# Output projections of a two-layer graph transformer in seven half-size products, and the attention of two batches taken together

## The chip, the cores and the metric

The kernel runs on one core of a Trainium2 chip. The metric is device time in microseconds (us), and lower is better. The engines are named as the profile names them: PE (TensorE, matrix products), PEld (its weight loads), DVE (VectorE), ACT (ScalarE), POOL (GpSimd) and SP (SyncE, which here issues every DMA). Every engine takes its instructions in the order in which the program lists them, and waits at each for the semaphores that it needs.

## The reference, cut to what matters

There are 128 batches of 128 nodes with 512 features, all in float32. Layer 0 is multi-head attention with 4 heads of 64 under an adjacency mask; layer 1 is a layer norm followed by attention with 8 heads of 64 under the mask with its diagonal set. Each layer adds its input to its output and normalises the sum.

```python
q, k, v = split_heads(x @ Wq), split_heads(x @ Wk), split_heads(x @ Wv)   # 4 heads (layer 0), 8 (layer 1)
sim = where(mask, einsum('bhid,bhjd->bhij', q, k) * scale, very_negative)
out = einsum('bhij,bhjd->bhid', softmax(sim), v)        # attention output, 256 or 512 wide
x = layernorm(x + out.reshape(B, N, INNER) @ Wo + bo)   # output product: 256 or 512 -> 512
```

The output product is the part that the change computes in another way. Per batch it multiplies 128 rows of 256 (layer 0) or 512 (layer 1) by a matrix with 512 columns.

## The kernel before, in words

**Groups and steps.** Two batches form a group g, and there are 64 groups. `step(s)` (L531) is called 67 times. In the steady state one step carries five groups' work at once: layer 0's q, k and v of group s (`product_0`, L337), layer 0's attention of group s-1, layer 1's q and k of group s-2 (`product("qk")`, L275), and layer 1's v and attention of group s-3 (`product("v")`). Within a step the attention is done twice, once per batch: `scores(k)` is called with k = 2s and k = 2s+1, and these two calls divide the step into a first and a second half.

**Products of two batches.** The projections to q, k and v use a seven-product scheme: the two batches' rows and the two halves of the columns make 2x2 blocks, and seven half-size products with sums of inputs and of weights take the place of eight. `sums` (L257) makes four sums of the inputs on POOL. Weight sums are made once. The products are numbered: 1, 6, 7 and 4 pile up in one PSUM bank ("a"), 5 and 3 in another ("f"), 2 has its own ("c"). Since a bank is read in between, the next product into it waits until DVE or ACT has read the one before it.

**Attention.** `scores` (L386) multiplies q and k into four PSUM banks (two per layer), POOL fills a tile `sm` with a very negative number (L410), DVE copies the scores into it under the mask (L412, two per layer; for layer 1 after merging the diagonal into the mask, L407) and takes the negative maximum of each row (L415). ACT takes the exponentials (`exps`, L424). `normalised` (L427) takes reciprocals of the sums on DVE (L432) and multiplies on POOL (L433). `blocks` (L436) transposes 32x32 blocks on DVE (L448) and sends them to DRAM, from where `probs_arrive` fetches them with four DMAs into their transposed place `pT`. `attend` (L458) multiplies with v and ACT copies the result to `aT` (L474).

**Output and norm.** `addend` (L476) adds the bias to the residual on POOL (in layer 1 after a scaling on ACT). `residual` (L487) makes the output product of one batch, with 512 columns (two matmuls in layer 0, four in layer 1), and DVE adds the addend (L499) and takes mean and variance (L501, L503); small POOL instructions make the root, and `norms` (L522) scales on DVE. Layer 1's result goes out by DMA. `turn` and `arrive` transpose a group's features by way of DRAM in the same way as the probabilities; `finish` (L245) and `in_order` (L235) put them in place on ACT, followed by the sums on POOL.

**What sets the order.** The tile framework's scheduling is off (`manual_schedule`): the order on each engine is that in which `step` calls these functions, and a helper that issues to DVE stands in DVE's queue where it was called. `exponentials` and `flush` empty lists of work put off, in the same way. [...]five rotate under the name "mm" (L50), three are fixed: "a", "a0" and a shared "f".

Of the kernel before, what the change touches and what calls it, by code (L numbers as in the profile page):

```python
# [27 lines left out]
def kernel(ctx: ExitStack, tc: tile.TileContext, x, adj, wq, wk, wv, wo, bo,  # L28
# [13 lines left out]
    four = ctx.enter_context(tc.tile_pool(name="four", bufs=4))  # L42
    dram = ctx.enter_context(tc.tile_pool(name="dram", bufs=2, space=bass.MemoryType.DRAM))
    ps_mm = ctx.enter_context(tc.tile_pool(name="ps_mm", bufs=5, space=PSUM))
# [20 lines left out]
    X, M = {}, {}  # L65

    def load(g):
        if g >= NG:
            return
        X[g] = four.tile([P, G, E], F32, tag="x", name=f"x_{g}")  # L70
        M[g] = four.tile([P, G, N], U8, tag="m", bufs=6, name=f"m_{g}")
        nc.sync.dma_start(X[g], x[g * G:(g + 1) * G].rearrange("b n e -> n b e"))
        nc.sync.dma_start(M[g], adj[g * G:(g + 1) * G].rearrange("b i j -> i b j"))
# [8 lines left out]
    mhalf = const.tile([P, 2], F32, name="mhalf")  # L82
# [25 lines left out]

    spare = []
    for tag, n in (("qk1", 4), ("v1", 2), ("xT1", 2), ("xs1", 2)):  # L110
        rows_n = one.tile([P, n, E], F32, tag=tag, name=f"raw_{tag}")
        spare.extend(rows_n[:, i] for i in range(n))

    def load_transposed(dst, src, name, scaled=0):
        rows, cols = src.shape
        raws = []
        for r in range(rows // P):
            if not spare:
                raw = three.tile([P, cols], F32, tag="h", bufs=7, name=f"{name}_{r}")
            else:  # L120
                raw = spare.pop(0)
            nc.sync.dma_start(raw, src[r * P:(r + 1) * P, :])
            raws.append(raw)
# [36 lines left out]
    def weight_sums():  # L160
        for w, ws in ((w1qk, wsqk), (w1v, wsv)):
            for c in range(KH):
                if w is w1qk:
                    b11, b12 = w[:, c, :, 0], w[:, c, :, 1]
                    b21, b22 = w[:, KH + c, :, 0], w[:, KH + c, :, 1]
                else:
                    b11, b12 = w[:, c, 0], w[:, c, 1]
                    b21, b22 = w[:, KH + c, 0], w[:, KH + c, 1]
                t2, t3, t4 = ws[:, 0, c], ws[:, 1, c], ws[:, 2, c]
                nc.vector.tensor_sub(t3, b22, b12)  # L170
                nc.vector.tensor_sub(b12, b12, b11)
                nc.vector.tensor_sub(t2, b22, b12)
                nc.vector.tensor_sub(t4, b21, t2)

    def weight_sums_0():
        b11, b12, b21, b22 = (w0[:, c:c + KH, h].rearrange("p c t f -> p c (t f)")
                              for c in (0, KH) for h in range(2))
        t2, t3, t4 = (ws0[:, i].rearrange("p c t f -> p c (t f)") for i in range(3))
# [4 lines left out]

    weight_sums_0()
    load_transposed(w1, w_qkv, "w_qkv", scaled=INNER[1])
    setup.append(turn_gamma_beta)
    load_transposed(wo1, w_out, "w_out")
    setup.append(weight_sums)

    WO = (wo0, wo1)  # L190
    RATIO, H, XT, QK, V, QKV = {}, {}, {}, {}, {}, {}
# [14 lines left out]
    TURNED, SCR, RAW = {}, {}, {}  # L206

    def turn(l, g, b):
        if not 0 <= g < NG:
            return  # L210
        if b == 0:
            TURNED[l] = one.tile([P, 4, G * KC * 32], F32, tag=f"turned{l}", name=f"turned{l}_{g}")
        src = X[g][:, b] if l == 0 else H[g, b]
        nc.vector.transpose(TURNED[l].rearrange("p a (b c i) -> p a b c i", b=G, c=KC)[:, :, b],
                            src.rearrange("p (c a i) -> p a c i", a=4, i=32))
        if b == G - 1:
            SCR[l] = put(TURNED[l], f"scr{l}_{g}")

    def arrive(l, g):
        if not 0 <= g < NG:  # L220
            return
        RAW[l] = one.tile([P, 4, G, KC, 32], F32, tag=f"raw{l}", name=f"raw{l}_{g}")
        fetch(RAW[l].rearrange("p a b c i -> p a (b c i)"), SCR[l])

    def first_transposed():
        xT = XT[0, 0] = one.tile([P, KC, T], F32, tag="xT0", name="xT0_0")
        for b in range(G):
            pt = mm_tile(f"xt_{b}")
            for c in range(KC):
                nc.tensor.transpose(pt[:, c * N:(c + 1) * N], X[0][:, b, c * P:(c + 1) * P], ident)  # L230
# [26 lines left out]
    def sums(l, g):  # L257
        xT = XT[l, g]
        xs = one.tile([P, 4, KH, N], F32, tag=f"xs{l}", name=f"xs{l}_{g}")
        a = xT.rearrange("p (h c) (b n) -> p b h c n", h=2, b=2)  # L260
# [6 lines left out]
        XS[l, g] = xs  # L267
# [69 lines left out]
    def product_0(g, *which):  # L337
# [5 lines left out]
        for i in which:  # L343
# [10 lines left out]
            elif first:  # L354
                tag = {"a": "a0", "f": "f"}[bank]
                ACC[0, bank] = ps_st.tile([P, 512], F32, tag=tag, name=f"{bank}0_{g}")
# [11 lines left out]
            if i in (1, 5, 6):  # L368
                e = one.tile([P, 512], F32, tag=("e5_0" if i == 5 else f"e{i}"), name=f"e0_{i}_{g}")
                EV[0, i] = e[:, :3 * P]  # L370
# [8 lines left out]
    SM, SUM, PT, AT, XB = {}, {}, {}, {}, {}  # L379
# [6 lines left out]
    def scores(k):  # L386
# [32 lines left out]
        exponentials(1)  # L419
# [16 lines left out]
    def blocks(k):  # L436
# [7 lines left out]
        pT = one.tile([P, 4, sum(HEADS), 32], F32, tag="pT", name=f"pT_{k}")  # L444
# [13 lines left out]
    def attend(k):  # L458
        both = members(k)
        if not both:  # L460
            return
        for l, g, b in both:
            K = HEADS[l] // 2
            pT = PT.pop((l, g, b))
            pm = mm_tile(f"av{l}_{g}_{b}")

            for h in range(HEADS[l]):
                s, kk = h % 2, h // 2
                o = pm[s * D:(s + 1) * D, kk * N:(kk + 1) * N]
                v = QKV[g][:, b, kk, 2, s * D:(s + 1) * D] if l == 0 else V[1, g][:, b, h * D:(h + 1) * D]  # L470
                nc.tensor.matmul(o.rearrange("p (a r) -> p a r", r=32), v, pT[:, :, s * K + kk, :],  # L471
                                 start=True, stop=True)
            AT[l, g, b] = two.tile([P, INNER[l]], F32, tag=f"aT{l}", name=f"aT{l}_{g}_{b}")
            nc.scalar.copy(AT[l, g, b], pm[:, :INNER[l]])  # L474

    def addend(l, k):  # L476

        for _, g, b in [m for m in members(k) if m[0] == l]:
            if l == 0:
                xin = X[g][:, b, :]  # L480
            else:
                xin = H.pop((g, b))
                nc.scalar.activation(xin, xin, AF.Copy, scale=RATIO.pop((g, b)))  # L483
            nc.gpsimd.tensor_tensor(xin, xin, (bias0, bias1)[l], op=ALU.add)  # L484
            XB[l, g, b] = xin

    def residual(l, k):  # L487
        for _, g, b in [m for m in members(k) if m[0] == l]:
            aT = AT.pop((l, g, b))
            nk = INNER[l] // P  # L490
            pm = mm_tile(f"o{l}_{g}_{b}")
            for c in range(nk):
                nc.tensor.matmul(pm, aT[:, c * P:(c + 1) * P], WO[l][:, c, :],  # L493
                                 start=(c == 0), stop=(c == nk - 1))
            if l == 0:
                y = three.tile([P, E], F32, tag="h", bufs=7, name=f"h_{g}_{b}")
            else:
                y = two.tile([P, E], F32, tag="y", name=f"y_{g}_{b}")
            nc.vector.tensor_add(y, pm, XB.pop((l, g, b)))  # L499
            st = three.tile([P, nc.vector.BN_STATS_DIM], F32, tag="st", name="st")  # L500
            nc.vector.bn_stats(st, y)  # L501
            mv = three.tile([P, nc.vector.BN_AGGR_DIM], F32, tag="mv", name=f"mv{l}_{g}_{b}")
            nc.vector.bn_aggr(mv, st)  # L503
            n = 2 - l
            ve = three.tile([P, 2], F32, tag="ve", name="ve")
            nc.gpsimd.tensor_scalar_add(ve[:, 0:1], mv[:, 1:2], EPS)  # L506
            if l == 0:


                nc.gpsimd.tensor_scalar(ve[:, 1:2], mv[:, 1:2], 1.0 + EPS, EPS * EPS,  # L510
                                        op0=ALU.mult, op1=ALU.add)
            r = three.tile([P, 2], F32, tag="rstd", name="rstd")
            nc.gpsimd.tensor_tensor(r[:, :n], ve[:, :n], mhalf[:, :n], op=ALU.pow)  # L513
            if l == 0:

                ratio = three.tile([P, 1], F32, tag="ratio", bufs=10, name=f"ratio_{g}_{b}")
                nc.gpsimd.tensor_scalar(ratio, ve[:, 1:2], r[:, 0:1], r[:, 1:2], op0=ALU.mult,
                                        op1=ALU.mult)
                RATIO[g, b] = ratio
            later.append(lambda: norms(l, g, b, y, mv, r))  # L520

    def norms(l, g, b, y, mv, r):  # L522
        n = 1 - l
        nc.vector.tensor_scalar(y, y, mv[:, 0:1], r[:, n:n + 1], op0=ALU.subtract, op1=ALU.mult)  # L524
        if l == 0:
            H[g, b] = y
        else:
            nc.sync.dma_start(out[g * G + b], y)


    def step(s):  # L531
# [6 lines left out]
        k = 2 * s  # L538
        scores(k)
        addend(0, k - 1)  # L540
        residual(1, k - 2)
        p("qk", 4, g=s - 3)
        exponentials()
        attend(k - 1)
        normalised(k)
        addend(1, k - 1)
        flush()
        turn(0, s + 1, 0)
        turn(0, s + 1, 1)
        product_0(s, 1, 5)  # L550
        p("", g=-1)
        blocks(k)
        arrive(0, s + 1)
        product_0(s, 2, 6)
        p("", g=-1)
        product_0(s, 3)
# [73 lines left out]
```

## Time and profile before

| | us |
|---|---|
| median of 3 runs (lowest, highest) | 2987.09 (2982.59, 2987.37) |
| the profiled execution, its own time | 2984.46 |
| its span, first to last instruction | 2982.70 |
| PE busy | 2920.0 (98%) |
| DVE busy | 1854.0 (62%) |
| POOL busy | 1567.4 (53%) |
| ACT busy | 1334.2 (45%) |
| TensorE clock granted (mean) | 0.994 |

The profile lists, for each group of instructions of one line and shape, how many there were, their busy time, the mean duration, and the idle time ahead of them with the engine that ended it. One float32 matmul shows as two records. Matmul records overlap in time, so the cost of one is read from start to start of neighbouring ones in the timeline, and not from its duration. In the steady state the two calls of `scores` start 45.14 us apart from step to step: from 145.58 us of the span (step 4) to 2854.3 us there are 60 such steps, the stretch ahead of them fills the pipeline, and the 128.4 us behind them drain it.

### The profile page before, as it was taken

The numbers are of one execution on the slowest core, as the hardware profiler recorded it, in microseconds if no ns is written. First come the engines' busy times: TensorE is split into PE (matmuls) and PEld (weight loads), VectorE is DVE, ScalarE is ACT, GpSimd is POOL, SyncE is SP. The second block draws the span as 40 slices with busy tenths as digits, with TensorE's granted clock in tenths as the row PEclk, the third lists the DMA queues.
The fourth block names the chain that finished last, engine by engine and source line by source line (L and its number), as shares of the span: only waits on it lengthen the run. The fifth ranks groups of instructions, "written<-read, shape, count | busy, mean of one in ns | idle before, by whom it ended". The sixth has DMA issues, their size and how long they took to land.

```text
span 2982.7 us, 59421 instructions
## 1 busy us (share of the span) xinstructions
PE 2920.0 (98%) x22089; PEld 2402.9 (81%) x22089; DVE 1854.0 (62%) x3291; ACT 1334.2 (45%) x4619; POOL 1567.4 (53%) x2055
## 2 busy tenths in 40 slices
PE   6899999999999999999999999999999999999997
PEld 5788888888888888888888888888888888888865
DVE  4466666666666666666656666666666666666654
ACT  2344444444444444444544444444444444444442
POOL 2455545545545555555555555455455455455543
PEclk8999999999999999999999999999999999999999
DMA  5454544544544544544544545545445445445332
GB/s 170 123 149 129 150 141 127 161 136 124 165 135 125 165 136 127 160 134 134 156 132 140 150 131 147 146 129 153 141 126 161 137 122 168 133 125 163 118 100 89
DMA packets 249136, 414.42 MB, mean 139 GB/s; under 512 B 41608, under 2 KB 181392, under 8 KB 248848
## 3 DMA queue, kind: packets, MB, share of 16 engines
q1 hardware_dynamic: 248848, 410.62, 46.3%
q8 instruction: 175, 2.87, 0.4%
q14 instruction: 113, 0.93, 0.1%
HBM read 209.72 MB, written 200.80 MB: 138 GB/s over the span
## 4 chain that ended last, share of the span: by engine, by line
PE 96%; DVE 1%; DMA 1%; ACT 1%; issue 0%; POOL 0%; SPq 0%; POOLq 0%; DVEq 0%; ACTq 0%
PE o L493 22%; PE qka L304 15%; PE a L361 12%; PE qkf L304 8%; PE va L304 8%; PE sc L400 6%; PE av L471 6%; PE f L361 6%; PE qkc L304 4%; PE vf L304 4%; PE c L361 3%; PE vc L304 2%; ACT sm L424 1%; DMA scrp<-turned 0%; DMA pT<-scrp 0%
## 5 line engine op out<-in xcount | busy, mean ns | idle before, releaser
L424 ACT ACTIVATE sm<-sm,nmax 128x128 f32<-128x128 f32 x1536 | 595.2, 389 | 618.6 <-DVE nmax L415 604.9
L493 PE MATMUL o<-wo,aT 128*128 128x512 f32 x1536 | 713.2, 600 | 10.0 <-ACT aT L474 10.0
L506 POOL TENSOR_SCALAR ve<-mv 128x1 f32<-128x1 f32 x256 | 57.0, 223 | 1133.0 <-DVE rec L432 798.8
L493 PEld LDWEIGHTS o<-wo,aT 128*128 128x128 f32 x1536 | 278.3, 191 | 269.3 <-issue 246.8
L433 POOL TENSOR_TENSOR sm<-sm,rec 128x512 f32<-128x512 f32 (+1 forms) x256 | 397.0, 1561 | 171.9 <-DVE rec L432 171.9
L412 DVE COPY_PREDICATED sm<-m,sc 128x512 f32<-128x512 uint8 (+1 forms) x512 | 271.0, 581 | 29.1 <-POOL sm L410 7.0
L424 ACT ACTIVATION_READ_ACCUMULATOR sm<-sm,nmax 128x1 f32 x1536 | 288.0, 187 | 0.0
L448 DVE STREAM_TRANSPOSE turned<-sm 128x512 f32<-128x512 f32 (+1 forms) x256 | 246.0, 965 | 45.0 <-POOL sm L433 45.0
L304 PE MATMUL qkf<-xs,w 128*128 128x128 f32 x2048 | 249.9, 275 | 0.1
L304 PE MATMUL qka<-xs,wsqk 128*128 128x128 f32 x2048 | 249.6, 275 | 0.0
L415 DVE TENSOR_REDUCE nmax<-sm 128x4 f32<-128x512 f32 (+1 forms) x256 | 244.0, 953 | 8.8
L304 PEld LDWEIGHTS qkf<-xs,w 128*128 128x128 f32 x2048 | 239.0, 192 | 0.6 <-POOL xs L266 0.4
L304 PEld LDWEIGHTS qka<-xs,wsqk 128*128 128x128 f32 x2048 | 239.0, 192 | 0.0
L524 DVE TENSOR_SCALAR h<-h,mv,rstd 128x512 f32<-128x512 f32 x128 | 70.0, 547 | 265.0 <-POOL rstd L513 265.0
L432 DVE RECIPROCAL rec<-total 128x4 f32<-128x4 f32 (+1 forms) x256 | 44.7, 175 | 296.6 <-ACT sm L424 296.6
L266 POOL TENSOR_TENSOR xs<-xT 128x256 f32<-128x256 f32 x256 | 186.0, 727 | 34.4 <-PE w_qkvt L129 14.5
L410 POOL MEMSET sm<- 128x512 f32 (+1 forms) x256 | 181.1, 735 | 1.4 <-DVE turned L448 1.3
L330 ACT COPY ev<-va 128x256 f32<-128x256 f32 x128 | 47.6, 372 | 298.7 <-PE va L304 298.7
L513 POOL TENSOR_TENSOR rstd<-ve,mhalf 128x2 f32<-128x2 f32 (+1 forms) x256 | 165.9, 648 | 21.3
L330 ACT COPY eqk<-qka 128x512 f32<-128x512 f32 x128 | 75.1, 587 | 214.4 <-PE qka L304 214.4
L484 POOL TENSOR_TENSOR h<-h,bias 128x512 f32<-128x512 f32 x128 | 162.7, 1271 | 7.0 <-ACT h L483 6.9
L484 POOL TENSOR_TENSOR x<-x,bias 128x512 f32<-128x512 f32 x128 | 162.2, 1267 | 0.0
(122 smaller groups left out, 5825.5 us busy)
## 6 DMA issues: line engine op xcount, KB each, us to landing
scrp<-turned SPq DMA_DIRECT2D x124, 768.0 KB, 3.3
pT<-scrp SPq DMA_DIRECT2D x496, 192.0 KB, 4.0
scr<-turned SPq DMA_DIRECT2D x127, 512.0 KB, 2.7
raw<-scr SPq DMA_DIRECT2D x508, 128.0 KB, 3.0
x<-in_x_dram SPq DMA_DIRECT2D x64, 512.0 KB, 4.2
out_dram<-y SPq DMA_DIRECT2D x128, 256.0 KB, 2.0
m<-in_adj_dram SPq DMA_DIRECT2D x64, 32.0 KB, 4.0
scrp<-turned SPq DMA_DIRECT2D x4, 512.0 KB, 3.2
```

The costliest lines, as they stand in the source:

```text
L266: nc.gpsimd.tensor_tensor(o, a0, a1, op=op)
L304: nc.tensor.matmul(o, lhsT, rhs, start=first and n == 0, stop=n == len(todo) - 1, skip_group_check=True)
L361: nc.tensor.matmul(acc[:, t * P:(t + 1) * P], lhsT, rhs, start=first and n == 0, stop=n == len(todo) - 1, skip_group_check=True)
L400: nc.tensor.matmul(ps[h % 2][:, h // 2, :], q_, k_, start=True, stop=True)
L410: nc.gpsimd.memset(sm, (NEG0, NEG1)[l])
L412: nc.vector.copy_predicated(sm[:, s], mask[:, None, :].to_broadcast([P, K, N]), ps[s][:, :K, :])
L415: nc.vector.tensor_reduce(nmax, sm, AX.X, ALU.max, negate=True)
L424: nc.scalar.activation(sm[:, s, k, :], sm[:, s, k, :], AF.Exp, bias=nmax[:, s, k:k + 1], accum_out=total[:, s, k:k + 1])
L433: nc.gpsimd.tensor_tensor(sm, sm, rec[:, :, :, None].to_broadcast([P, 2, K, N]), op=ALU.mult)
L448: nc.vector.transpose(t[:, :, lo:hi, :], sm)
L484: nc.gpsimd.tensor_tensor(xin, xin, (bias0, bias1)[l], op=ALU.add)
L493: nc.tensor.matmul(pm, aT[:, c * P:(c + 1) * P], WO[l][:, c, :], start=(c == 0), stop=(c == nk - 1))
```

## The change

It has five parts.

1. **Output products in seven.** `out_product` takes the place of the matmuls in `residual`. It makes seven products of 256 columns for a group (one matmul each in layer 0, two in layer 1), with sums of the attention outputs (`out_sums`, four POOL instructions per layer and group) and weight sums made once at the start (`weight_sums_out`). DVE adds each product into the residual where it lies, half a row at a time. There are seven such additions per layer and group, in place of two of full width.
2. **Two batches in one go.** `attend` is called once per step, for both batches of groups s-2 and s-4; layer 0's two batches share one PSUM tile and one ACT copy. `pT` has two buffers. `addend`, the roots and the ratios are made for two batches at a time (one instruction where there were two).
3. **In place.** The input, the layer-0 output and the result of a group share one tile `R` (six buffers); layer 1's last scaling moves from DVE to ACT (`norms_1`), and one DMA per group writes the result. The load of the next group moves from the middle of a step to its start.
4. **PSUM.** The rotating "mm" banks go from five to four, and "f0" becomes a fixed bank of its own.
5. **Order.** `product_0`'s seventh and fourth products come ahead of the second `scores`; of v's seven products three (1, 5, 2) come ahead of it and four behind it, where it was five and two. The product 2 of v is now the last on PE ahead of the second `scores`, and in DVE's queue its addition, layer 0's norm of both batches (`flush`) and both transposes of `turn(1)` stand directly ahead of those scores' masks. The output products are strewn between the others, with their additions in DVE's queue at the same places. There is one step more (68).

```diff
-    ps_mm = ctx.enter_context(tc.tile_pool(name="ps_mm", bufs=5, space=PSUM))
+    ps_mm = ctx.enter_context(tc.tile_pool(name="ps_mm", bufs=4, space=PSUM))
...
+    def out_product(l, g, *which):
...
+        for i in which:
+            left = {1: aT[:, 0, :hk], 2: aT[:, 0, hk:], 3: so[:, 3], 4: aT[:, 1, hk:], 5: so[:, 0],
+                    6: so[:, 1], 7: so[:, 2]}[i]
+            right = {1: w[:, :hk, :EH], 2: w[:, hk:, :EH], 3: w[:, hk:, EH:], 4: ws[:, 2],
+                     5: w[:, :hk, EH:], 6: ws[:, 0], 7: ws[:, 1]}[i]
+            bank, first = INTO[i]
...
+            for c in range(hk):
+                nc.tensor.matmul(acc, left[:, c], right[:, c], start=first and c == 0, stop=c == hk - 1,
+                                 skip_group_check=True)
+            b, h = {1: (0, 0), 2: (0, 0), 6: (0, 1), 3: (0, 1), 5: (1, 1), 7: (1, 1), 4: (1, 0)}[i]
+            part = R[g][:, b, h * EH:(h + 1) * EH]
+            nc.vector.tensor_add(part, acc, part)
...
-    def attend(k):
+    def attend(s):
+        for l, g in ((0, s - 2), (1, s - 4)):
...
+    def out_sums(l, g):
...
+        halves_sums(so, AT[l, g].rearrange("p b (h c) n -> p b h c n", h=2))
...
-    def norms(l, g, b, y, mv, r):
-        nc.vector.tensor_scalar(y, y, mv[:, 0:1], r[:, n:n + 1], op0=ALU.subtract, op1=ALU.mult)
+    def norms_0(g, mv, root):
+        for b in range(G):
+            nc.vector.tensor_scalar(R[g][:, b], R[g][:, b], mv[:, b, 0:1], root[:, 1, b:b + 1],
+                                    op0=ALU.subtract, op1=ALU.mult)
+    def norms_1(g, shift, root):
+        for b in range(G):
+            nc.scalar.activation(R[g][:, b], R[g][:, b], AF.Identity, bias=shift[:, b:b + 1],
+                                 scale=root[:, 0, b:b + 1])
+        nc.sync.dma_start(out[g * G:(g + 1) * G].rearrange("b n e -> n b e"), R[g])
```

The whole of the new `step`, in the order of its calls (`p("", g=-1)` calls, which only take setup work, are left out):

```python
load(s + 1); scores(k); exponentials(1); addend(0, s - 2)          # k = 2 * s
p("qk", 4, g=s - 3); product_0(s, 1); exponentials()
attend(s); out_sums(0, s - 2); normalised(k)
product_0(s, 5); product_0(s, 2); addend(1, s - 4)
out_product(0, s - 2, 1, 5, 2, 6); product_0(s, 6)
out_product(0, s - 2, 3); stats(0, s - 2, 0); out_product(0, s - 2, 7); product_0(s, 3)
out_product(0, s - 2, 4); product_0(s, 7); stats(0, s - 2, 1)
p("v", 1, 5, g=s - 3); blocks(k); product_0(s, 4); p("v", 2, g=s - 3)
flush(); turn(1, s - 2); arrive(1, s - 2); probs_arrive(k)
k += 1
scores(k); p("v", 6, g=s - 3); exponentials(1); out_sums(1, s - 4)
out_product(1, s - 4, 1); p("v", 3, g=s - 3); exponentials()
out_product(1, s - 4, 5, 2); p("v", 7, g=s - 3); normalised(k)
out_product(1, s - 4, 6); p("v", 4, g=s - 3)
finish(s - 2); turn(0, s + 1); blocks(k)
out_product(1, s - 4, 3); stats(1, s - 4, 0); out_product(1, s - 4, 7)
arrive(0, s + 1); probs_arrive(k); p("qk", 1); p("qk", 5)
out_product(1, s - 4, 4); stats(1, s - 4, 1); p("qk", 2)
in_order(s + 1); p("qk", 6); flush(); p("qk", 3, 7)
```

The old `step` called, from its second `scores` on:

```python
scores(k); addend(0, k - 1); p("v", 7, g=s - 3); residual(1, k - 2)
exponentials(); p("v", 4, g=s - 3); attend(k - 1); normalised(k); addend(1, k - 1); flush()
finish(s - 2); product_0(s, 7); blocks(k); residual(0, k - 1); product_0(s, 4)
in_order(s + 1); p("qk", 1); probs_arrive(k); flush(); turn(1, s - 1, 0)
p("qk", 5); p("qk", 2, 6); p("qk", 3, 7)
```

## The prediction

> **What bounds the kernel now.** I read the page's engine shares and chain first, then the waits of the steady state, then one step in the windows and timeline. From the page:
>
> ```profile
> PE 2920.0 (98%) x22089; PEld 2402.9 (81%) x22089; DVE 1854.0 (62%) x3291; ACT 1334.2 (45%) x4619; POOL 1567.4 (53%) x2055
> PE 96%; DVE 1%; DMA 1%; ACT 1%; issue 0%; POOL 0%; SPq 0%; POOLq 0%; DVEq 0%; ACTq 0%
> L493 PE MATMUL o<-wo,aT 128*128 128x512 f32 x1536 | 713.2, 600 | 10.0 <-ACT aT L474 10.0
> ```
>
> PE is the bound: it carries 96% of the chain, and between 200 and 2800 us the view of PE's waits is empty. The windows view of one step's two halves:
>
> ```profile
> core 0: us, PE busy (x) PEld busy (x) DVE busy (x) ACT busy (x) POOL busy (x), PEclk, DMA share, GB/s
> 1364.63:1386.11 21.48, 21.48 (x158) 17.34 (x157) 13.91 (x25) 9.00 (x34) 7.37 (x11) 1.00 0.37 117
> 1386.11:1409.77 23.66, 23.66 (x189) 19.89 (x188) 14.76 (x27) 11.82 (x38) 17.11 (x22) 1.00 0.59 164
> ```
>
> A step is 45.14 us of PE without a gap, so what PE loses or waits per step counts 60 times. How near the others are shows the timeline behind the second scores (start, duration, engine; PE's and DVE's rows):
>
> ```profile
> 1386.11 0.71 PE L400 MATMUL sc<-qkv 64*128 64x128 f32 x8
> ...
> 1386.92 0.78 DVE L412 COPY_PREDICATED sm<-m,sc 128x256 f32<-128x256 uint8 x2
> ...
> 1388.61 3.60 PE L493 MATMUL o<-wo,aT 128*128 128x512 f32 x8
> ...
> 1390.13 1.22 DVE L415 TENSOR_REDUCE nmax<-sm 128x8 f32<-128x1024 f32 x1
> ...
> 1391.27 0.41 DVE L335 TENSOR_TENSOR v<-va,ev 128x256 f32<-128x256 f32 x1
> ...
> 1392.05 1.03 PE L304 MATMUL va<-wsv,xT 128*128 128x256 f32 x4
> ...
> 1394.89 1.25 DVE L524 TENSOR_SCALAR y<-y,mv,rstd 128x512 f32<-128x512 f32 x1
> ```
>
> v's product 4 (PE, 1392.05) goes into the bank that DVE's addition of product 7 must first have read. That ends at 1391.68: PE is covered by 0.37 us only, and with a short DVE queue.
>
> **The skill.** The Trainium skill, "TensorE: Matmul & The Clock Gate", Back-to-back issue gap, makes the gap proportional to the columns plus 2.5 ns. The trace agrees in form: 429 ns from start to start at 512 columns, 216 at 256, 112 at 128, about twice its bf16 figure. The same page's opening table says that VectorE, ScalarE and GpSimdE take their queues strictly in order; agreed: every DVE row here stands in program order. "SBUF — State Buffer", Who interferes with whom: a DVE tensor_scalar in its two-port mode, and a DVE operation with two SBUF inputs against a POOL operation that reads, lock each other out for a whole instruction. The trace agrees for the first: L524's y takes 0.51 us ahead of a POOL multiplication, and 1.25 (last row above) behind one. No row shows the second.
>
> **PE's work per step.** Removed: 24 records of 512 columns, 24 x 0.429 = 10.3 us. Added: seven products of 1 + 2 matmuls, two records each, 42 x 0.216 = 9.07 (pitch of v's 256-column records: product 1 to 5, 1381.70 to 1382.56, four records in 0.86). Gain 1.25. One `attend` less saves a change of tile shape: the groups entering and leaving it take 0.95 for 0.86 and 1.44 for 1.34 us, so 0.2. PE's work becomes 45.14 - 1.45 = 43.7.
>
> **DVE's queue behind the second scores.** T is their start on PE. Before, the first mask copy starts at T+0.81. After, DVE must first add v's product 2, which PE finishes at T: T+0.25 to 0.65; then two norms of 0.55 and two transposes of 0.71. The mask copy starts at T+3.25, 2.45 later. The second negative maximum ended at T+5.24 before, now T+7.7. Then five additions of 0.43 (o1, v3, o5, o2, v7) where before one stood: v7's ends at T+9.7. PE reaches v's product 4 after scores 1.53, v6 0.97 and six products of 0.864 at T+7.7. It waits **2.1**, most of it already at o6, which needs o1's addition.
>
> Next late is o7, behind o6's addition. That stands behind the reciprocal of layer 1, which waits for ACT: T+7.7, exponentials 3.2 (the 16 ACT rows 1391.44 to 1394.63), reciprocal to 11.3, addition to 11.7. PE is there at 9.8 + 2 x 0.864 = 11.5: **0.3**. Then PE does o7, qk1, qk5 (0.864 + 2 x 1.79) to 16.25, and o4 needs o7's addition, behind `turn(0)` 1.35, blocks 0.70 + 1.25, o3's addition 0.41, statistics 0.95, 0.41: T+16.8. **0.6**. From o4 on (o4, qk2, 6, 3, 7: 8.0) nothing is late. Second half: 3.0.
>
> First half, from the first scores at 0 (durations from the rows of this step): PE reaches o1 at 10.4 after scores 1.54, qk4 1.79, product_0's 1 1.42, both batches' attention 2.85, product_0's 5 and 2 2.78. o1 needs ACT's copy: maxima end at 5.24, ACT starts the exponentials at 5.5 behind product_0's copy, 3.2, then its own copy 0.6, so 9.3; o5 at 10.8 needs POOL's first sum at 9.8. Covered by 1.0. Then o4 needs o7's addition, which stands behind o3's and 0.95 of statistics: **0.35**. POOL's multiplication ends at 14.6; DVE's second statistics (behind product_0's 7, which PE ends at 17.9) at 19.7 and the blocks at 21.7, just ahead of T = 21.9. So DVE is free at T, and the count above starts from PE. The roots (L506, L510 and a power of four elements, between 0.72, the row of two, and 1.1, twice the row of one; I take 1.0) end at 21.2, ahead of the norms.
>
> The lock: `addend(0)` is one POOL instruction of 2 x 1.27 us beside the mask merge; if DVE waits for it, ACT's copies for o1 come up to 1.9 later, and PE loses 0 to 0.8. The norms meet POOL's memsets and sums: 0 to 0.5. I take 0.35 of these 0 to 1.3, as the starts differ by tenths. Sum: 43.7 + 3.0 + 0.35 + 0.35 = **47.4 us per step**, +2.26, times 60 = +136.
>
> **What is hidden.** Output sums (4 x 0.46 and 4 x 0.73, the first an estimate from L266's 0.73 at 256 and L484's 1.27 at 512 elements) and longer addends: POOL is busy 24.5 of 45 us, and o1, o2 need no sum; uncovered 5 us. Layer 1's norm on ACT (2 x 0.73): ACT has 24 us idle. One bank fewer: each "mm" bank is read well ahead of its next use, except v2's, read at T+0.65 where scores want it at T+0.55. DMAs: probabilities are stored at T+15, transposed features ahead of them in SP's queue; last landing about T+24.5 (store 3.3, four issues 1.73, landing 4.0), `attend` is near T+30. The features for `finish` land about T+12 (six us from first issue to use at 1390.62) where ACT is free at T+11.4: qk1 waits 0.6, but then o4 doesn't. Load and result move 512 KB each in SP's queue while that is idle. Fill and drain: weight sums are behind the setup's DMAs; the last group adds four sums (3 us), a double addend and its statistics, +7 (0 to 15).
>
> **Sum.** 2982.7 + 136 + 7 = 3126 span; 1.8 outside it as before; the median lies 2.6 above the profiled execution: **3130**.
>
> **Rivals.** (a) PE stays the only bound: step 43.7, 2987 - 1.45 x 60 + 7 = 2907, faster. For it: DVE is only some 70% busy, and the products are strewn so as to leave room. Against it: DVE's order is fixed and o1's addition can't pass the exponentials' maxima. It decides where DVE is late by less than 1.45 us per step; I count 3.35. (b) The lock costs in full, +0.95 more per step: 3187; or the transposed features or probabilities land 2 us later than their rows, as loads and stores now meet, with about 1.5 more: 3220. For it: DMA is at 0.59 share in the second half. Against: the memset only writes, and the landings above are of a loaded queue. (c) Waits and gain cancel within 0.2%: a stall of just 1.4 to 1.6.
>
> **Chances.** The likeliest (3090 to 3170): 0.63. (b) 0.23, of which 0.07 above 3200. (a) 0.11. (c) 0.03. 0.2% is about what a measurement of this kernel tells from no change. Range 3000 to 3200: below it lie (a) and (c), above it 0.07. Slower 0.86, same 0.03, faster 0.11.
>
> **What would show it.** Right: 256-column output records at 216 ns, a step of 47 us in which PE's waits name DVE's r (output additions) and v ahead of o6, v4, o7 and o4, and nearly none in the last 8 us; the first mask copy 3.2 us behind the second scores. Wrong: PE without waits (then (a)); PE waiting for ACT's aT or POOL's sums in the first half with mask merges far above 0.28 us, or for DMA (then (b)). What would make it wrong is above all a DVE that catches up ahead of T, or additions much shorter than 0.41 us.

## The result, and the profile after

| | before | after |
|---|---|---|
| median, us (lowest to highest; 4 runs each) | 2985.59 (2982.59 to 2987.37) | 3163.26 (3159.20 to 3165.31) |
| span of the profiled execution, us | 2982.7 | 3157.3 |
| one steady step, mean of 58, us | 45.15 | 47.67 |
| granted TensorE clock, mean | 0.994 | 0.989 |

The changed kernel is slower: the ratio is 1.0595, with a 95% interval of 1.0576 to 1.0613. The forecast was 3130, with a range of 3000 to 3200.

The page of the changed kernel, with engine shares, the chain that ended last, and the groups of the output products and of their additions:

```profile
PE 2927.3 (93%) x23241; PEld 2631.7 (83%) x23241; DVE 2035.6 (64%) x3811; ACT 1427.7 (45%) x4683; POOL 1721.3 (55%) x2247
PE 26%; DVE 25%; DMA 20%; ACT 12%; POOL 7%; issue 5%; SPq 5%; ACTq 0%; DVEq 0%; POOLq 0%
L404 PE MATMUL oa<-wso,so 128*128 128x256 f32 x768 | 218.0, 393 | 83.3 <-DVE r L408 83.3
L408 DVE TENSOR_TENSOR r<-oa,r 128x256 f32<-128x256 f32 x512 | 209.4, 409 | 131.8 <-PE oa L404 117.9
```

PE's share of the chain was 96% and is 26%. DVE, DMA and ACT now stand in it too. PE is still shown as 93% busy, since a record that is held up counts as busy, and DVE is at 64%. The waits of PE between 200 and 2800 us, where the kernel before has no row (us in total, times, longest):

```profile
PE oa L404 <- DVE r L408: 72.1, 108, 1.1
PE qka L312 <- ACT eqk L338: 31.0, 36, 1.8
PE oa L404 <- ACT aT L511: 18.4, 55, 0.7
```

The view counts only the gap that is left between two records. The records of a group that waits also stretch, so the whole loss is read from start to start. The timeline of the second half of the step that starts at 1115.02 us, PE's rows (start, duration, idle before):

```profile
1137.48 0.71 PE L432 MATMUL sc<-qkv 64*128 64x128 f32 x8
1138.02 1.26 PE L432 MATMUL sc<-qk 64*128 64x128 f32 x16
1139.22 1.13 PE L312 MATMUL va<-wsv,xs 128*128 128x256 f32 x4
...
1143.64 1.03 PE L312 MATMUL va<-wsv,xs 128*128 128x256 f32 x4
1145.74 1.10 PE L404 MATMUL oa<-wso,so 128*128 128x256 f32 x4 [1.07 <-DVE r L408]
1146.97 1.13 PE L312 MATMUL va<-wsv,xT 128*128 128x256 f32 x4
1147.94 1.03 PE L404 MATMUL of<-wo,so 128*128 128x256 f32 x4
1149.24 1.10 PE L404 MATMUL oa<-wso,so 128*128 128x256 f32 x4 [0.27 <-DVE r L408]
1150.17 1.95 PE L312 MATMUL qka<-xT,w 128*128 128x128 f32 x16
```

T is 1137.48. Four records of 256 columns cost 0.86 where nothing waits. From v7 (1143.64) to o6 it is 2.10, so 1.24 is lost ahead of o6. From o6 to v4 it is 1.23 (0.37 lost), and from o3 to o7 1.30 (0.44 lost). DVE's rows of the same stretch, and the mask merge near the start of the step:

```profile
1117.45 1.91 DVE L439 TENSOR_TENSOR m<-m,eye 128x128 uint8<-128x128 uint8 x1
...
1137.65 0.42 DVE L343 TENSOR_TENSOR v<-vc,ev 128x256 f32<-128x256 f32 x1 [0.89 <-PE vc L312]
1137.99 1.74 DVE L570 TENSOR_SCALAR r<-r,mv,root 128x512 f32<-128x512 f32 x2
1139.65 1.29 DVE L223 STREAM_TRANSPOSE turned<-r 128x512 f32<-128x512 f32 x2
1140.87 0.73 DVE L444 COPY_PREDICATED sm<-m,sc 128x256 f32<-128x256 uint8 x2
...
1144.04 1.22 DVE L447 TENSOR_REDUCE nmax<-sm 128x8 f32<-128x1024 f32 x1
1145.18 0.41 DVE L408 TENSOR_TENSOR r<-oa,r 128x256 f32<-128x256 f32 x1
...
1146.50 0.42 DVE L343 TENSOR_TENSOR v<-va,ev 128x256 f32<-128x256 f32 x1
...
1148.72 0.37 DVE L408 TENSOR_TENSOR r<-oa,r 128x256 f32<-128x256 f32 x1
```

The chain of the prediction can be read off: v2's addition, two norms and two transposes stand ahead of the first mask copy, which starts at T+3.39 (T+0.81 before, T+3.25 predicted). The second negative maximum ends at T+7.8, and only then comes o1's addition, for which o6 waits on PE. v7's addition ends at T+9.4 (predicted 9.7), and o6's, for which o7 waits, follows the reciprocals.

The two norms take 1.74 us for 1.09 before (2 x 547 ns). Beside them POOL shows

```profile
1137.18 1.42 POOL L442 MEMSET sm<- 128x512 f32 x2
1138.56 0.89 POOL L275 TENSOR_TENSOR so<-aT 128x256 f32<-128x256 f32 x1
```

The first norm starts inside the memsets and ends 0.28 us behind their end; the second starts inside the addition and ends 0.28 us behind its end. The last section comes back to this.

Two losses lie elsewhere. In the first half the merge takes 1.91 us beside this row of POOL:

```profile
1116.85 2.36 POOL L527 TENSOR_TENSOR r<-r,bias 128x1024 f32<-128x1024 f32 x1
```

The merge was 281 ns in the mean before (L407). Here it starts 0.60 us behind the addend and ends 0.15 us behind its end. Everything behind it is later, down to ACT's copy `aT`, for which layer 0's o1 waits. The other loss is at the end of a step. Of the 60 steady steps 39 are short (about 47.2 us, all under 48) and 21 are long (48.0 to 48.9). This is ACT and then PE at the end of a long one, the step that starts at 1400.99:

```profile
1439.93 0.58 ACT L338 COPY eqk<-qkf 128x512 f32<-128x512 f32 x1 [1.19 <-PE qkf L312]
1445.77 1.14 ACT L249 COPY xT<-raw 128x512 f32<-128x512 f32 x2 [5.25 <-DMA raw<-scr]
1446.82 0.58 ACT L338 COPY eqk<-qka 128x512 f32<-128x512 f32 x1
```

```profile
1444.16 1.95 PE L312 MATMUL qkf<-xs,w 128*128 128x128 f32 x16
1447.54 2.02 PE L312 MATMUL qka<-xs,wsqk 128*128 128x128 f32 x16 [1.43 <-ACT eqk L338]
```

qk7 needs its bank "a" read by ACT's copy of qk6. That copy stands behind `in_order`'s copies, and these wait for the features to land. ACT is idle for 5.25 us with the copy that PE wants in its queue.

### The profile page after: what moved, and what is told of

The parts are those of the page before. It is cut to its first block, busy times and chain, and to the rows that moved or that the text cites. A ratio compares the mean times of both kernels' runs of the same rounds, so it can differ in the third digit from the quotient of the medians.

```text
span 3157.3 us, 62734 instructions
## 1 busy us (share of the span) xinstructions
PE 2927.3 (93%) x23241; PEld 2631.7 (83%) x23241; DVE 2035.6 (64%) x3811; ACT 1427.7 (45%) x4683; POOL 1721.3 (55%) x2247
## 4 chain that ended last, share of the span: by engine, by line
PE 26%; DVE 25%; DMA 20%; ACT 12%; POOL 7%; issue 5%; SPq 5%; ACTq 0%; DVEq 0%; POOLq 0%
ACT sm L455 10%; DMA scr<-turned 9%; PE a L368 8%; DMA raw<-scr 8%; DVE sm L444 6%; DVE nmax L447 6%; POOL xs L275 6%; PE oa L404 5%; SPq L214 5%; DVE turned L223 4%; DVE m L439 4%; DVE r L570 3%; DMA pT<-scrp 3%; PE f L368 3%; PE of L404 2%
## 5 line engine op out<-in xcount | busy, mean ns | idle before, releaser
L464 POOL TENSOR_TENSOR sm<-sm,rec 128x512 f32<-128x512 f32 (+1 forms) x256 | 373.1, 1467 | 410.6 <-DVE rec L463 410.6
L275 POOL TENSOR_TENSOR so<-aT 128x128 f32<-128x128 f32 (+1 forms) x256 | 161.9, 633 | 431.8 <-ACT aT L511 431.8
L527 POOL TENSOR_TENSOR r<-r,bias 128x1024 f32<-128x1024 f32 x128 | 301.3, 2354 | 4.9 <-ACT r L526 4.9
L404 PE MATMUL oa<-wso,so 128*128 128x256 f32 x768 | 218.0, 393 | 83.3 <-DVE r L408 83.3
L408 DVE TENSOR_TENSOR r<-oa,r 128x256 f32<-128x256 f32 x512 | 209.4, 409 | 131.8 <-PE oa L404 117.9
L404 PEld LDWEIGHTS oa<-wso,so 128*128 128x128 f32 x768 | 133.6, 190 | 146.2 <-issue 130.2
L479 DVE STREAM_TRANSPOSE turned<-sm 128x512 f32<-128x512 f32 (+1 forms) x256 | 234.5, 953 | 8.3 <-POOL sm L464 8.0
L404 PE MATMUL of<-wo,so 128*128 128x256 f32 x768 | 215.8, 390 | 4.3 <-POOL so L275 4.3
L249 ACT COPY xT<-raw 128x512 f32<-128x512 f32 x126 | 71.7, 616 | 281.4 <-DMA raw<-scr 281.4
L547 POOL TENSOR_SCALAR ve<-mv 128x2 f32<-128x2 f32 x128 | 28.1, 220 | 295.7 <-DVE mv L539 295.7
```

Of the source, the lines that this page charges most:

```text
L275: nc.gpsimd.tensor_tensor(o, a0, a1, op=op)
L404: nc.tensor.matmul(acc, left[:, c], right[:, c], start=first and c == 0, stop=c == hk - 1, skip_group_check=True)
L408: nc.vector.tensor_add(part, acc, part)
L464: nc.gpsimd.tensor_tensor(sm, sm, rec[:, :, :, None].to_broadcast([P, 2, K, N]), op=ALU.mult)
L479: nc.vector.transpose(t[:, :, lo:hi, :], sm)
L527: nc.gpsimd.tensor_tensor(R[g], R[g], (bias0, bias1)[l][:, None, :].to_broadcast([P, G, E]), op=ALU.add)
```

## The experiments

Each ratio is to runs of the kernel before on the same chip, whose medians beside e1 to e9 lie between 2984.22 and 2985.09. e1 to e5 have two runs each, e6 18, e7 17, e8 four and e9 twelve.

| run | edit | median, us | ratio (95% interval) | steady step, us |
|---|---|---|---|---|
| (the changed kernel) | | 3163.26 | 1.0595 (1.0576 to 1.0613) | 47.67 |
| e1 | mask merges ahead of the other masks | 3117.48 | 1.0448 (1.0418 to 1.0479) | 47.00 |
| e2 | `in_order` behind qk6 | 3177.45 | 1.0649 (1.0619 to 1.0680) | 47.90 |
| e3 | v2 behind the second scores | 3091.42 | 1.0361 (1.0331 to 1.0391) | 46.55 |
| e4 | layer 0's norm left out | 3061.97 | 1.0262 (1.0233 to 1.0292) | 46.19 |
| e5 | full-width output products | 3320.07 | 1.1122 (1.1085 to 1.1159) | 50.36 |
| e6 | four moves together | 2980.43 | 0.9985 (0.9978 to 0.9992) | 44.77 |
| e7 | e6 and two moves more | 2977.31 | 0.9976 (0.9968 to 0.9984) | 44.73 |
| e8 | e6 with full-width output products | 3014.71 | 1.0097 (1.0080 to 1.0113) | 45.46 |
| e9 | e7 with earlier features in the fill | 2989.42 | 1.0011 (1.0003 to 1.0020) | 44.77 |

### e1: the merges ahead of the masks

```diff
+        merged = {}
+        for l, g, b in both:
+            if l == 1:
+                merged[g] = two.tile([P, N], U8, tag="m1", name=f"m1_{g}_{b}")
+                nc.vector.tensor_tensor(merged[g], M[g][:, b, :], eye, op=ALU.max)
         for (l, g, b), ps in zip(both, made):
             K = HEADS[l] // 2
-            mask = M[g][:, b, :]
-            if l == 1:
...
+            mask = merged[g] if l == 1 else M[g][:, b, :]
```

> The mask merge of layer 1 (DVE, two SBUF inputs) is issued ahead of layer 0's mask copies, and so ahead of the long POOL addition. Theory (the two lock each other out, 1.9 us, and PE pays 0.5 us per step at the first output product): merge back to 0.28 us, no wait of PE for aT, about 3163 - 0.5 x 60 = 3133 us. Rival (the wait is only relabelled, ACT or POOL is as late without the lock): 3160 or more.

Measured: 3117.48, a step of 47.00 (0.67 less, where the theory had 0.5). The group of the merge, and PE's waits between 200 and 2800 us:

```profile
L438 DVE TENSOR_TENSOR m<-m,eye 128x128 uint8<-128x128 uint8 x128 | 44.3, 346 | 0.0
```

```profile
PE oa L404 <- DVE r L408: 69.3, 110, 1.0
PE qka L312 <- ACT eqk L338: 32.4, 37, 1.9
```

The merge's mean falls from 1047 ns to 346, the row of `aT` is gone, and the two other rows stay as they were. So the merge beside POOL's addend is what makes o1 wait, and it costs more than the gap of 0.33 that the view of waits gives it: the groups around it lose 0.70 from start to start (below), and the edit brings 0.67.

### e2: the copies of the features behind qk6

```diff
         p("qk", 2)
-        in_order(s + 1)
         p("qk", 6)
+        in_order(s + 1)
         flush()
```

> ACT's copy of qk product 6 is issued ahead of the copies that wait for the transposed features' DMA. Theory (PE's last product of a step waits for that copy, 35 us in all): 3163 - 35 = 3128 us. Rival (the late features come back at the next step's start, since POOL's fill of the score tile stands behind the sums that wait for them, and the mask copies then wait for it): 3145 to 3165, with a wait of the first mask copy for POOL above 1 us.

Measured: 3177.45, slower than the changed kernel. PE's waits, and a row of DVE's:

```profile
PE oa L404 <- DVE r L408: 72.1, 108, 1.1
PE oa L404 <- ACT aT L511: 71.2, 54, 1.7
```

```profile
DVE sm L444 <- POOL sm L442: 70.5, 55, 2.4
```

The wait of qk7 is gone, and 52.8 us come in its place at `aT` (18.4 to 71.2). The sums of the next group are now late on POOL, the fill of the first scores' tile stands behind them, and DVE's first mask copy waits for that fill (12.3 us before the edit, 70.5 with it). This was the rival, though the time is 12 us above its range. In this order of POOL's queue the late landing is paid for either at qk7 or at the next masks. e6 moves the fill as well.

### e3: v2 behind the second scores

```diff
         product_0(s, 4)
-        p("v", 2, g=s - 3)
         flush()
...
         out_product(1, s - 4, 1)
+        p("v", 2, g=s - 3)
         p("v", 3, g=s - 3)
```

> v's product 2 moves on PE from just ahead of the second scores to behind output product 1, so DVE's norm and transposes no longer stand behind its addition. Theory (PE's second half waits because DVE's queue reaches the second scores late): first mask copy about 1.2 us earlier, waits at output products 6 and 7 and at v's 4 shrink by as much, 3163 - 75 = 3088 us. Rival (four rotating PSUM banks, or the DMA landings, set the step): within 15 us of 3163.

Measured: 3091.42, a step of 46.55 (1.12 less), close to the theory's 3088. PE's waits:

```profile
PE qka L312 <- ACT eqk L338: 28.3, 31, 1.7
PE va L312 <- DVE v L343: 25.9, 56, 0.5
PE oa L404 <- ACT aT L511: 18.8, 56, 0.7
PE oa L404 <- DVE r L408: 7.6, 49, 0.2
```

With v2's addition gone from the front of DVE's queue, and its 0.86 us of PE work put between the scores and o6, the wait for the output additions falls from 72.1 to 7.6. Half a microsecond per step comes back at v's products, behind v7's addition. The prediction's main stall is a matter of place: PE had 0.86 too little to do there, and DVE 0.4 too much.

### e4: layer 0's norm left out

```diff
     def norms_0(g, mv, root):
-        for b in range(G):
-            nc.vector.tensor_scalar(R[g][:, b], R[g][:, b], mv[:, b, 0:1], root[:, 1, b:b + 1],
-                                    op0=ALU.subtract, op1=ALU.mult)
+        pass
```

> Leaves out the scaling by layer 0's norm (two DVE instructions per step, 1.75 us); all else is as in the changed kernel. Theory (DVE's queue): the second half's DVE chain is 1.7 us shorter, and PE's waits there (2.05 us per step) nearly vanish: 3163 - 100 = 3063 us. Rival (banks or DMA): within 15 us of 3163.

Measured: 3061.97, a step of 46.19 (1.48 less), as the theory had it. The norms took 1.74 us ahead of the mask copy (1137.99 above), and 1.48 of it comes back. So most of the time that DVE saves ahead of the second masks is PE's time, and the stall behind the second scores is DVE's queue, not the work of PE.

### e5: full-width output products in the new order

The seven products are undone alone. Each batch gets one product of 512 columns (two matmuls in layer 0, four in layer 1) and one full addition; the sums are left out, and the rest of the order stays.

```diff
-        out_product(0, s - 2, 1, 5, 2, 6)
+        out_full(0, s - 2, 0)
...
-        out_product(0, s - 2, 3)
+        out_full(0, s - 2, 1)
...
-        out_product(1, s - 4, 1)
+        out_full(1, s - 4, 0)
...
-        out_product(1, s - 4, 5, 2)
+        out_full(1, s - 4, 1)
...
-        out_product(1, s - 4, 6)
...
```

> Undoes the seven output products alone: one product of 512 columns per batch, two additions of full width per layer and group, no output sums; everything else of the changed kernel stays (two batches at once, in place, four rotating banks, the new order). PE has 1.25 us more per step, DVE about 3 us less. Theory (the order of DVE's queue ahead of the second scores is what makes PE wait): v's 4 still waits about 2 us, step 48.0, about 3185 us. Rival (the fourteen small additions are what makes DVE late): waits in the second half gone, step 46.5, about 3095 us.

Measured: 3320.07, a step of 50.36. Both theories missed, by 135 and 225 us. PE's waits:

```profile
PE qka L310 <- ACT eqk L336: 61.2, 48, 2.3
PE qka L310 <- ACT xT L258: 49.1, 51, 1.1
PE of L415 <- DVE sm L451: 29.1, 51, 0.6
PE va L310 <- DVE v L341: 26.4, 51, 0.5
PE of L415 <- ACT aT L518: 15.4, 47, 0.6
```

Two of the five waits are the output products' own (L415): for a bank that the mask copies have yet to read, and for `aT`. The larger ones are at qk. The edit is no clean undo: in layer 1 both products (3.44 us each) stand ahead of v7 and v4, where o1, o5 and o2 (2.6 us together) stood, and nothing is left behind v4 to give ACT and the landing time. The products also draw on the four "mm" banks. So the run says little of the products themselves: exchanging them alone leaves an order that does not fit the large ones. What the small ones are worth has to be asked in another way (e8).

### e6: four moves together

e1, e2 and e3 together, and with them what e2 lacked: POOL fills the next scores' tile ahead of the next group's sums.

```diff
         p("qk", 2)
-        in_order(s + 1)
         p("qk", 6)
+        fill(k + 1)
+        in_order(s + 1)
         flush()
...
-            nc.gpsimd.memset(sm, (NEG0, NEG1)[l])
+    def fill(k):
+        for l, g, b in members(k):
+            FILLED[l, g, b] = filled(l, g, b)
```

> Seven products kept; four changes of order at once: mask merge first, v's product 2 behind output product 1, the copies that wait for the transposed features behind the copy of qk product 6, and the next scores' fill ahead of the sums on POOL. Theory (the waits are independent and add up: 0.67 and 1.12 us per step as measured alone, and 0.5 for the last two together): step 45.4, about 3026 us. Rival (one wait is taken over by the next): 3060 or more.

Measured: 2980.43, a step of 44.77, and one row of PE's waits:

```profile
PE vc L312 <- DVE sm L455: 3.1, 3, 1.5
```

The sum of the single edits underrated it by 0.6 us per step, or 46 us in the time. Each single run still showed waits that are gone here (e3 at qk7, at v's products and at `aT`). How the 0.6 is shared among the four moves was not tried, and the fill was never moved alone. All of the 2.5 us that the change cost per step was the order of the calls, and its parts (products in seven, two batches in one go, in place, four banks) stay. The short list of waits does not mean that PE loses nothing: from start to start 1.3 us of the 44.77 are still lost, nearly all at output products and the groups beside them. In the time the kernel is only 0.15% faster than before, since it loses in the fill and the drain what it wins in the steps: against before, the first scores of step 3 start 10.3 us later (112.7 for 102.4), the 63 steps from there to the last take 20.6 less, and the drain takes 6.1 more.

### e7: two moves more

```diff
         out_product(0, s - 2, 4)
-        product_0(s, 7)
         stats(0, s - 2, 1)
+        product_0(s, 7)
...
-        p("v", 3, g=s - 3)
+        p("v", 7, g=s - 3)
         exponentials()
+        p("v", 3, g=s - 3)
         out_product(1, s - 4, 5, 2)
-        p("v", 7, g=s - 3)
```

> As the repairs, and layer 0's second statistics ahead of the addition of product_0's 7, and v's product 7 and its addition ahead of v's 3, so that v's 4 is released earlier. Theory: blocks, norms and transposes start about 0.5 us earlier and v's 4 waits 0.5 less: step 44.9, about 2995 us. Rival (ACT's exponentials set the second half from here on): as the repairs.

Measured: 2977.31, with a step of 44.73 where e6 has 44.77. Against before it is 0.24% faster (0.16 to 0.32), the fastest kernel here. e6 and e7 ran beside the same runs of before, and e7 is faster than e6 by 3.1 us in the median (2.5 in the mean, 95% interval 1.2 to 3.9). The theory's 0.5 us per step for v4 did not come as a gain. v4 is no longer late, as it said, but another product is:

```profile
PE oa L404 <- DVE r L408: 17.0, 58, 0.3
```

This is o7, which loses 0.53 from start to start where it lost 0.18 in e6. What makes it later stays open.

### e8: the seven products alone, in the repaired order

As e5, but from e6, with the two products of a layer in the banks that the half-size products had used, and layer 1's second one behind v4, at the place of o3.

> This is the version with four moves, with part 1 alone undone: one full-width output product per batch (four records of 512 columns in layer 0, eight in layer 1), each in a bank of its own that the half-size products used before, the first batch's at the place of product 1 and the second batch's at the place of product 3; no sums of attention outputs and no weight sums. Theory (the seven products are worth their PE time where PE is the bound, 24 x 0.429 - 42 x 0.216 = 1.25 us per step): the step becomes 44.77 + 1.25 = 46.0, and the time 2980 + 60 x 1.25 = 3055. Rival (DVE's additions eat part of the gain: four full ones of 0.7 us take the place of fourteen of 0.41, so that the 0.9 us of waits that are left go away): a step of 45.1 to 45.3, about 3005.

Measured: 3014.71, a step of 45.46 (0.69 more than e6). PE's only wait:

```profile
PE va L310 <- DVE v L341: 30.2, 57, 1.0
```

The result lies between the theories. Full width costs 10.30 us of PE per step, as computed. The seven products cost 9.98 from start to start in e6 and not 9.07, since DVE's additions still hold them up here and there; that is 0.32 of the difference. The rest, 0.37, is a balance: v4's wait for v7's addition costs the full-width version 0.80 from start to start, and the groups beside the output products lose 0.43 in e6 that they do not lose here. So in these two orders the seven products are worth 34 us of time (3014.71 - 2980.43; 1.0097 and 0.9985 of before), about half of what their PE time says. How much of that a better order for the full products would take back was not tried. The sums of the weights at the start cost nothing visible: without them step 3 starts at 113.7, with them at 112.7.

### e9: the features earlier in the fill

```diff
+        if s < 3:
+            turn(0, s + 1)
+            arrive(0, s + 1)
         product_0(s, 3)
...
         product_0(s, 4)
+        if s < 3:
+            in_order(s + 1)
         flush()
```

Behind step 2 the three calls stay where they were.

> This is the version with six moves, and one more for the fill alone: in steps 0 to 2 the transposes of the next group's features, their way through DRAM, ACT's copies and POOL's sums stand ahead of the second half of the step, in the place of behind it. In the steady state nothing changes. Theory (the longer fill is PE waiting for ACT's copies of the features, 20.0 us in two waits for layer 0 and 9.3 in one for layer 1): two thirds of the 20 go, the step 3 starts some 12 us earlier, and the time is 2977 - 12 = 2965. Rival (the features are late for another reason, the load of the group or the landing of what is fetched): 2972 or more.

Measured: 2989.42, slower than e7. The steps are unchanged (44.77), but step 3 starts at 121.7 us (111.8 in e7). PE's waits up to 130 us, the largest ones of the fill:

```profile
PE qka L312 <- ACT xT L260: 11.4, 1, 11.4
PE av L517 <- DMA pT<-scrp: 9.9, 1, 9.9
...
PE c L368 <- DVE wo L140: 8.0, 1, 8.0
...
PE a L368 <- ACT xT L249: 4.5, 1, 4.5
```

The wait for layer 0's features fell from 20.0 to 4.5, that for layer 1's went from 9.3 to 11.4, and two new ones came: for the first probabilities (9.9) and for DVE's copies of the output weights (8.0), which stand behind sums of weights in DVE's queue. The theory is wrong: the features were what PE waited for, and not what the fill was bound by. What bounds it stays open.

## Why the prediction was right, and where it was off

The likeliest case came in: the mechanism, the place and nearly the size of the step. The range held the time, which lies 33 us above the number and inside the likeliest case's own range. That the step came within 0.3 us is in part luck: terms that were put too low add 1.6 us, and terms that were put too high, PE's own work among them, take 1.3 away. The table sets the prediction's terms against the loss from start to start, the mean of 58 steps of the changed kernel, each against the same group where nothing waits. Where there are several numbers, they belong to groups that follow each other and are held up by the same queue.

| PE's loss per step, us | predicted | measured |
|---|---|---|
| o6 and v4, behind the additions of o1 to v7 | 2.1 | 1.23 + 0.37 + 0.10 |
| o7, behind o6's addition | 0.3 | 0.44 + 0.07 |
| o4 of layer 1, behind o7's addition | 0.6 | 0 |
| o4 of layer 0 | 0.35 | 0.27 |
| the lock, seen at o1 of layer 0 | 0.35, of 0 to 1.3 | 0.70 |
| second scores, behind v2's bank | 0 | 0.21 |
| qk7, behind ACT's copy of qk6 | 0 | 0.82 |
| sum | 3.7 | 4.2 |
| step | 47.4 | 47.67 |

**PE's own work** was predicted at 43.7 us. 47.67 less 4.2 is 43.5. The records of 256 columns follow at 216 ns (0.86 for four), as the row of v's products had said. Rival (a), PE as the only bound, is out.

**What was to show it** showed it, but for two points: v is not named in PE's waits, because v4's loss lies in stretched records, and the last 8 us of a step are not free of waits in the long steps. What was named as the sign of rival (b) came too: PE waits for `aT` in the first half, with a merge far above 0.28 us.

**DVE's queue behind the second scores** was the step that carried the forecast. It stands, and three edits show it from three sides: less ahead of the masks (e4), one addition and one product moved (e3), and all moves together (e6). The term of 2.1 was 0.4 too large: v7's addition ended at T+9.4 for 9.7, and 0.21 of PE's delay fell in the scores already. The first mask copy was within 0.14 of its place by luck. The norms took 0.56 more than reckoned from start to start, which is the lock, and v2's addition and the transposes 0.3 less.

**o4 of layer 1** lost nothing for a predicted 0.6. o7's addition ended at 1153.6, ahead of o4's start at 1153.75. The prediction had stacked `turn(0)`, blocks, o3's addition and statistics ahead of it in full, and the stack was about 0.6 shorter than its sum.

**The lock** was placed rightly and put too low. The Trainium skill, "SBUF — State Buffer", section Who interferes with whom, says that a DVE instruction with two SBUF inputs contends with a POOL instruction that reads, and the kernel before had no row that showed it. Here the merge takes 1.91 us for 0.28 beside the addend, and e1 shows that the loss at o1 hangs on it. The norms were held up as well, by 0.65 (1.74 for 1.09), and they stand in the queue ahead of the second masks. At e4's rate (1.48 of the step for 1.74 of norms) that is about 0.55 of the 1.70 lost at o6 and v4. This is an estimate, since no run takes the lock of the norms away alone. The lock then cost about 1.25 in all, near the top of the 0 to 1.3 that the prediction gave it. So rival (b)'s first case, the lock in full, came true beside the likeliest case, and DVE's queue without the lock cost less than was reckoned.

**qk7** is the step that failed: the prediction held that from o4 on nothing is late, and put 0 where 0.82 was lost. It followed the landings to their users, found `finish` and `attend` covered, and had the features for `in_order` in none of its sums; it did not ask what stands behind `in_order`'s copies in ACT's queue. That is ACT's copy of qk6, for which PE waits. The Trainium skill, "TensorE: Matmul & The Clock Gate", opening table, says that ScalarE takes its queue strictly in order, and the 5.25 us of ACT's idle time in the long step agree. Rival (b) had named features or probabilities that land late, but as another case and at 1.5 us per step; it came as 0.82 beside everything else. In the short step the four fetches of the features land 3.5 us after issue (median), in the long one 4.2. What makes them longer in some steps stays open.

**Fill and drain** were put at +7 (0 to 15) outside the 60 steps. From the spans, 3157.3 - 2982.7 = 174.6, of which 60 x 2.52 = 151 are the steps and 23 are outside: step 3 starts 11.7 us later (114.1 for 102.4), the drain behind the last first scores takes 6.0 more (53.5 for 47.5), and the rest are the three steps that the 60 leave out. The drain is as predicted. The fill is not: two rows of PE's waits up to 115 us,

```profile
PE a L368 <- ACT xT L249: 19.7, 2, 12.6
PE qka L312 <- ACT xT L260: 10.7, 1, 10.7
```

show where PE stands: behind the first scores of steps 1 and 2 (7.1 and 12.6) and behind the second scores of step 2 (10.7). `product_0` is now all in the first half, and in step 1 the second half has no PE work but its scores. That this order makes the fill longer is argued, and e9, which moved the features, did not bear it out. Of the 33 us by which the number was low, the steps are 60 x 0.27 = 16, and the fill most of the rest.

## What to carry to other kernels

Where one engine is the bound, cutting its work into smaller pieces adds places at which the engine that reads the pieces can hold it up. Follow that engine's queue to each bank's next use, and put enough other work of the bound engine between a product and the next one into its bank. A landing is hidden only if it is also early for what stands behind its user in the same queue, since e2, which only put qk6's copy ahead of it, merely moved the wait. With the fill moved ahead of the sums too (e6), PE no longer waits for it. When single repairs give little, try them together: here four moves brought 183 us (3163.26 to 2980.43), where e1 and e3 alone brought 46 and 72 and e2 cost 14 (the fourth was not run alone).

## What the runs showed of the hardware that was not expected

- A 128x128 merge of bytes on DVE with both inputs in SBUF takes 1.91 us, almost seven times its 0.28, if a POOL addition of 128x1024 (2.36 us) started 0.60 us ahead of it. It ends 0.15 us behind POOL's instruction.
- POOL instructions also hold up a norm (tensor_scalar on DVE, 128x512, float32), and it doesn't matter here whether they read. A norm took 0.547 us before. Of the changed kernel's 128 norms 63 take about 0.88 and end 0.25 to 0.30 us behind the end of a memset, which reads nothing, and 62 take about 0.94 and end as far behind an addition. In e3 and e6 the first norm of a pair starts ahead of the memsets and takes 0.547, while the second is caught by one and takes 0.88. The prediction had held against a full lock that the memset only writes. No run takes the memset away alone.
- In the page's idle columns a group that waits looks cheaper than it is: o1's gap ahead of it is 0.33 us, and the groups around it lose 0.70 from start to start.
